# Layer 1 of a graph network on one core: TensorE in the order of tracing, and the attention bias moved behind the division

## Chip, cores and metric
The kernel runs on one core of a Trainium2 chip. The metric is device time in microseconds (us) from launch to end; lower is better. Beside the runs there is one execution under the hardware profiler, whose page and trace are quoted. PE is the matrix engine TensorE (PEld its weight loads), DVE is VectorE, ACT is ScalarE, POOL is GpSimd, SP is SyncE, which here only issues transfers.

## The reference, cut to what matters
Two layers work on x of shape 32 x 512 x 256 (32 batches of 512 nodes) with an integer adjacency adj of 32 x 512 x 512. Each has a graph part and a feed-forward part, each added to x after a layer norm. The change touches only layer 1:

```python
# graph part: attention over the adjacency, 4 heads of 64; adj is 0 or 1
h = einsum('bnd,hde->bhne', layernorm(x), W)
weight = leaky_relu(e_src + e_dst), or -1e9 where adj == 0
attention = softmax(weight)
dst = einsum('bhij,bhje->bhie', attention, h) + bias
out = relu(dst) + h
out = (out - mean(out)) / sqrt(var(out) + 1e-6) * ln_gamma + ln_beta
x = x + out
# feed-forward part
sw = softmax((layernorm(x) @ W_x.T @ W_slice.T + ...) / temp)    # 8 heads of 64 slices
st = slices: sum over nodes of fx * sw, over the sum of sw
ot = a state-space scan over the 64 slices (convolutions, silu, softplus, decay matrices)
x = x + (ot spread back through sw) @ out_w.T + out_b
```

The weights of an attention row sum to one after the division, so the bias may be added to the values before the weighted sum or to the divided result after it.

## The kernel before
The program runs layer 0 (`layer0_sorted`) and then layer 1 (`layer1_plain`); a second pair of functions follows under a condition that is false for these inputs. Instructions are recorded by Python generators. A scheduler then places them on each engine: it takes an instruction when its inputs are ready by its own model of time, with the order of recording as the priority. So the order on an engine can differ from the order in which the code was traced.

Layer 1 takes 32 batches, two to a group, 16 groups. Two streams are woven together when they are recorded. One is `mixer(g)`, the feed-forward part of a group: `slices` for its first and its second batch, then `tokens`, `scan`, and `unslice` for both. The other is `attentions()`, which runs two batches ahead: `attention(b)` woven with `prepare(b + 1)`. The loop at the end (L1589 to L1597) advances the attention by credits: each step of `mixer` yields a weight `want`, and every full credit (`want * PACE`) runs one step of `attentions`. `STEPS` (L890) is the number of steps of `prepare`; it enters both `woven` and `PACE`.

`prepare(b)` gathers x by four indirect transfers issued from POOL (L1154), normalises it into the buffer of the values hv (ACT, L1133, after the statistics on DVE, L1126, and a power on POOL, L31), transposes it on PE (x3T, L1142, copied out by ACT, L1143) and multiplies it with the weights (hp, L1180, four tiles). ACT copies each tile to ht (L1186) and forms exponentials. POOL then adds the bias for all four tiles, from ht into hv (L1189), and DVE multiplies hv by an exponential in four steps (L1202). The logits of the rows are transposed (minep, L1193), written to memory and read back as four broadcast tiles `own` through SP (L1197, L1200). It also turns the adjacency into a mask (maskp L1084 on PE, cast by DVE L1085).

`attention(b)` forms the weights `att` on DVE (L1213), sums them with the values on PE (avp L1249, adp L1254: a "turn" is one row tile of all four heads), copies the sums out, transposes them back (dp, bp, L1232) and divides on DVE (L1275). `norm(b, av)` follows in three pieces: relu plus h (L1290), sum (L1292) and mean, subtraction (L1294), square on ACT (L1296), sum (L1298) and small steps (L1299), a power on POOL (L1300), multiplication by gamma (L1301) and by that power (L1303), and the addition to x (L1304).

`slices(b)` transposes x (x4T), computes logits (lgp, L1335, four tiles) and their exponential on ACT (L1336), normalises them on DVE (sw: L1337, L1340, L1341, L1342), and sums x over them on PE (yTp, L1347: two banks c of four tiles t, t inside c); swp (L1352) transposes sw. `tokens` and `scan` are one dependent chain: uTp, rnp, xp (L1400), bcp (L1409), dtp, zp (L1393); softplus and convolutions on DVE and ACT with several function tables; then gp (L1487), segp (L1491), xtp, qp, yp (L1517), yTp (L1527), oTp (L1535), vp (L1557); `unslice` computes outp (L1567), adds it to x (L1569) and writes the output. PSUM tiles of layer 1 share two tags of four banks, "any" and "pv".

Of the kernel before, what the change touches and what calls it, by code (L numbers as in the profile page):

```python
# [19 lines left out]
P = 128  # L20
N = 512
D = 256
NT = N // P
# [841 lines left out]
def layer1_plain(tc, ident, eps, x2s, ranks, adj, w, out, over, ps):  # L865
# [3 lines left out]
    nc = tc.nc  # L869
    B = adj.shape[0]  # L870
    SEG = B // len(x2s)
    GB = 2
    AH, _, HO = w["W"].shape
# [13 lines left out]
    HE = HO + 1  # L887
    AP = AH // 2
    TURNS = AP * NT + 6
    STEPS = 15  # L890
    WANTED = 68
    AHEAD = 3
    ATT = 2 * (AHEAD + 2) + AP + 1
# [7 lines left out]
    with ExitStack() as ctx:  # L901
# [246 lines left out]
        def prepare(b):  # L1148

            while b >= AHEAD_X and b - AHEAD_X not in stored:  # L1150
                yield True
            xt = xs[b] = sb.tile([P, NT, D], F32, tag="x", name=f"x{b}", bufs=AHEAD_X)
            for t in range(NT):
                nc.gpsimd.indirect_dma_start(  # L1154
                    out=xt[:, t, :], out_offset=None, in_=x2s[b // SEG],
                    in_offset=bass.IndirectOffsetOnAxis(
                        ap=ranks[:, b * NT + t : b * NT + t + 1].bitcast(U32), axis=0))

            hv = sb.tile([P, NT, AH, HE], F32, tag="hv", name=f"hv{b}")
            xn = hv.rearrange("p t h e -> p (t h e)")[:, : NT * D].rearrange("p (t d) -> p t d", t=NT)  # L1160
            edged = masks(b) if b not in masked else range(3)
            for i, _ in enumerate(edged):
                if i < 3 or b not in masked:
                    yield
                if i == 2:
                    normed(xt, xn, f"c{b}")
                    nc.gpsimd.tensor_add(xt, xt, beta.unsqueeze(1).to_broadcast([P, NT, D]))
                    yield
            mask = masked.pop(b)
            xnT = yield from turned(xn, "x3T", f"x3T{b}")  # L1170
            yield


            ht = sb.tile([P, NT, AH * HO], F32, tag="ht", name=f"ht{b}")
            other = sb.tile([P, NT, AH], F32, tag="other", name=f"other{b}")
            mine = sb.tile([P, AH, NT], F32, tag="mine", name=f"mine{b}")
            for t in range(NT):
                ph = psum("any", f"hp{b}_{t}")
                for c in range(DC):
                    nc.tensor.matmul(ph[:, : AH * (HO + 2)], xnT[:, c, t * P : (t + 1) * P], wa[:, c, :],  # L1180
                                     start=c == 0, stop=c == DC - 1)
                d = ph[:, AH * HO : AH * HO + AH]
                nc.scalar.activation(mine[:, :, t], ph[:, AH * (HO + 1) : AH * (HO + 2)], AF.Exp, scale=1.0 - SLOPE)
                nc.scalar.activation(hv[:, t, :, HO], d, AF.Exp)
                nc.scalar.activation(other[:, t, :], d, AF.Exp, scale=SLOPE - 1.0)
                nc.scalar.copy(ht[:, t, :], ph[:, : AH * HO])  # L1186
                yield

            nc.gpsimd.tensor_add(hv[:, :, :, :HO], ht.rearrange("p t (h e) -> p t h e", h=AH),  # L1189
                                 abias.rearrange("p (h e) -> p h e", h=AH).unsqueeze(1).to_broadcast([P, NT, AH, HO]))  # L1190
            yield
            pt = psum("any", f"minep{b}")
            nc.tensor.transpose(pt[: AH * NT, :P], mine.rearrange("p h t -> p (h t)"), ident)  # L1193
            row = sb.tile([AH * NT, P], F32, tag="turned", name=f"turned{b}", bufs=1)
            nc.scalar.copy(row, pt[: AH * NT, :P])
            own_row = dr.tile([AH, N], F32, tag="own", name=f"ownd{b}")
            nc.sync.dma_start(own_row.rearrange("h (t p) -> (h t) p", p=P), row)  # L1197
            own = [wide("own", f"own{b}_{h}", AH + 1) for h in range(AH)]
            for h in range(AH):
                nc.sync.dma_start(own[h], own_row[h].partition_broadcast(P))  # L1200
            for t in range(NT):
                nc.vector.tensor_mul(hv[:, t, :, :HO], hv[:, t, :, :HO], hv[:, t, :, HO:].to_broadcast([P, AH, HO]))  # L1202
            ready[b] = mask, ht, hv, other, own
            yield

# [10 lines left out]
        def attention(b):  # L1216

            mask, ht, hv, other, own = ready[b]
            xt = xs[b]
            av = sb.tile([P, NT, AH, HO], F32, tag="av", name=f"av{b}", bufs=1)  # L1220
            turns = [(q, j) for j in range(NT) for q in range(AP)]

            def begin(b, n):
                q, j = turns[n]
                if (b, 2 * q, j) not in weighed:
                    weigh(b, q, j)

            def back(src, kind):

                dst = psum("pv", f"{kind}{b}")  # L1230
                for t in range(NT):
                    nc.tensor.transpose(dst[:, t * P : (t + 1) * P], src[:, t * P : (t + 1) * P], ident)  # L1232
                return dst

            for n in range(AHEAD):
                begin(b, n)
            pv = [psum("pv", f"avp{b}_{q}") for q in range(AP)]
            for i, (q, j) in enumerate(turns):
                if i + AHEAD < len(turns):
                    begin(b, i + AHEAD)  # L1240
                elif b + 1 in ready:
                    begin(b + 1, i + AHEAD - len(turns))

                if q + 1 == AP:
                    ends = dict(start=j == 0, stop=j == NT - 1)
                    for p in range(AP):
                        for k in range(2 * HO // HW):
                            h, e = 2 * p + k * HW // HO, k * HW % HO
                            nc.tensor.matmul(pv[p][k * HW : (k + 1) * HW, :], hv[:, j, h, e : e + HW],  # L1249
                                             weighed[b, h, j], **ends)  # L1250
                    if j == 0:
                        pd = psum("pv", f"adp{b}")
                    for h in range(AH):
                        nc.tensor.matmul(pd[h * HW : (h + 1) * HW, :], hv[:, j, h, HO:].to_broadcast([P, HW]),  # L1254
                                         weighed.pop((b, h, j)), **ends)
                yield
                if unfinished and i != 2:
                    next(unfinished[0], None)
                    yield
                    if i > 2:  # L1260
                        unfinished.pop()
            dT = wide("att", f"adT{b}", ATT)
            nc.scalar.copy(dT, pd)
            vT = [wide("att", f"avT{b}_{q}", ATT) for q in range(AP)]
            for q in range(AP):
                nc.scalar.copy(vT[q], pv[q])
            yield
            dt = back(dT, "dp")
            rs = sb.tile([P, NT, AH], F32, tag="rs", name=f"rs{b}")
            nc.vector.tensor_scalar_max(rs, dt.rearrange("p (t h e) -> p t h e", t=NT, h=AH)[:, :, :, 0], 1e-30)  # L1270
            nc.vector.reciprocal(rs, rs)
            for q in range(AP):
                bt = back(vT[q], f"bp{q}_")
                heads = slice(2 * q, 2 * q + 2)
                nc.vector.tensor_mul(av[:, :, heads, :], bt.rearrange("p (t h e) -> p t h e", t=NT, h=2),  # L1275
                                     rs[:, :, heads].unsqueeze(3).to_broadcast([P, NT, 2, HO]))
                yield
            unfinished.append(norm(b, av))

# [293 lines left out]
        def mixer(g):  # L1573
            uT = sb.tile([P, KC, GB * G], F32, tag="uT", name=f"uT{g}", bufs=1)
            yT = sb.tile([P, DC, H, GB, G], F32, tag="yT", name=f"yT{g}", bufs=1)
            rn = sb.tile([P, GB, KC], F32, tag="rn", name=f"rn{g}")
            sws = []
            for j in range(GB):
                sws.append((yield from slices(g * GB + j, j, yT, rn)))
            yield 3  # L1580
            tokens(g, yT, rn, uT)
            v = yield from scan(g, uT)
            yield 2
            for j in range(GB):
                unslice(g * GB + j, sws[j], v[:, j])
                yield 2
# [1 line left out]

        ahead = attentions()  # L1589
        credit = 0.0  # L1590
        for g in range(B // GB):
            for want in mixer(g):
                credit += want * PACE
                while credit >= 1.0:
                    credit -= 1.0
                    if next(ahead, True):
                        credit = 0.0  # L1597


        flags = over[:, 2 * AH + 3 :]  # L1600
# [639 lines left out]
```

## Time and profile before

| what | value |
|---|---|
| runs | 4453.05, 4452.75, 4458.42 us; median 4453.05 |
| the profiled execution's own time | 4459.08 us |
| its span, first to last instruction | 4456.4 us, mean granted PE clock 0.948 |
| PE busy | 3922.0 us, 88% |
| PEld busy | 2470.6 us, 55% |
| DVE busy | 3347.2 us, 75% |
| ACT busy | 2291.6 us, 51% |
| POOL busy | 1718.8 us, 39% |
| transfers | 474.21 MB, mean 106 GB/s |
| last piece of layer 0 on PE, first of layer 1 | 2363.84 and 2384.94 us |

The profile has a page with busy times, the span in 40 slices, and the costliest groups of instructions. Further views of the same trace are the table of waits (who stood still for whom), the timeline (instructions in order, equal neighbours merged, with the idle time before a piece and what ended it in brackets), and the busy time of each engine within chosen stretches. A PE count of the profile is twice the number of matmuls in f32, since each matmul leaves two records; transposes through f32 leave one. A group of layer 1 lasts about 126 us.

### The profile page before, as it was taken

Reading aid. Unit: us, or ns where it says so; the run is one execution under the profiler, and the core shown is the slowest. Engines: PE = TensorE matmul, PEld = TensorE weight load, DVE = VectorE, ACT = ScalarE, POOL = GpSimd, SP = SyncE. Lnnn points to the kernel's source line nnn. Section 1 sums busy time; section 2 is a strip of 40 time slices with the busy share of each in tenths; the row PEclk is TensorE's granted clock in tenths of the full one; section 3 lists DMA queues with packets and bytes.
Section 4 is the critical chain, followed back from the end, with each engine's and each line's share of the span. In section 5 each row is a group of like instructions: output and inputs, shape, how many; then the busy total and the mean of one; then the engine's idle time right before and its main releaser. Section 6 shows DMA issues by size and latency. Waiting matters only on the chain.

```text
span 4456.4 us, 57911 instructions
## 1 busy us (share of the span) xinstructions
PE 3922.0 (88%) x20311; PEld 2470.6 (55%) x20311; DVE 3347.2 (75%) x7008; ACT 2291.6 (51%) x4756; POOL 1718.8 (39%) x2036
## 2 busy tenths in 40 slices
PE   5568898899988999888997899999999999999987
PEld 4454565566656656545554455555555555555555
DVE  6668887897788987877766777767677877778763
ACT  3345565566564665556654544544545444454433
POOL 2357644664446644454314232332222232332220
PEclk8679999999999999989998999999999999999998
DMA  5546543664436543564422111111111111111100
GB/s 133 160 144 223 190 130 122 210 200 139 156 117 213 187 147 129 162 201 167 138 81 67 36 53 57 56 48 58 51 43 42 53 55 55 58 48 58 41 15 16
DMA packets 235107, 474.21 MB, mean 106 GB/s; under 512 B 38299, under 2 KB 114075, under 8 KB 234804
## 3 DMA queue, kind: packets, MB, share of 16 engines
q0 software_dynamic: 98688, 315.94, 22.2%
q1 hardware_dynamic: 136116, 154.46, 11.0%
q8 instruction: 162, 2.65, 0.2%
q14 instruction: 141, 1.16, 0.1%
HBM read 413.16 MB, written 57.16 MB: 106 GB/s over the span
## 4 chain that ended last, share of the span: by engine, by line
DVE 34%; PE 32%; DMA 11%; issue 9%; POOL 9%; ACT 5%; SPq 0%; POOLq 0%; DVEq 0%; ACTq 0%
DVE att L1213 5%; DVE acc L637 4%; PE clsp L623 3%; PE avp L1249 3%; PE po L652 3%; PE gatep L623 3%; DMA rows<-table,xs 2%; PE yTp L1347 2%; DVE sw L1337 2%; DVE sw L1342 2%; DVE best L598 2%; DMA rows<-table,tops 2%; DVE sst L1340 2%; DMA best<-table,xs 2%; PE xp L1400 1%
## 5 line engine op out<-in xcount | busy, mean ns | idle before, releaser
L623 PE MATMUL clsp<-xnT,wc 128*128 128x512 f32 x1024 | 520.8, 627 | 49.7 <-ACT cls L625 37.6
L623 PE MATMUL gatep<-xnT,wg 128*128 128x512 f32 x1024 | 499.8, 607 | 10.5 <-ACT gate L625 7.7
L652 PE MATMUL po<-wd,acc 128*128 128x256 f32 x2048 | 455.4, 381 | 6.1 <-DVE acc L641 3.8
L1213 DVE SCALAR_TENSOR_TENSOR att<-own,other,mask 128x512 f32<-128x512 f32 x512 | 392.9, 796 | 79.0 <-DMA own<-ownd 79.0
L652 PEld LDWEIGHTS po<-wd,acc 128*128 128x128 f32 x2048 | 388.3, 191 | 72.1 <-issue 9.2
L598 DVE SCALAR_TENSOR_TENSOR best<-rows,xs,best 128x1024 f32<-128x1024 f32 x212 | 274.4, 1295 | 121.9 <-ACT best L592 76.4
L637 DVE SCALAR_TENSOR_TENSOR acc<-past,fld,acc 128x512 f32<-128x512 f32 x448 | 345.7, 775 | 24.9 <-ACT past L636 16.9
L632 ACT ACTIVATE acc<-tz,fld 128x512 f32<-128x512 f32 x256 | 198.8, 777 | 269.3 <-PE tz L630 240.1
L623 PEld LDWEIGHTS gatep<-xnT,wg 128*128 128x128 f32 x1024 | 196.0, 196 | 252.3 <-issue 197.9
L636 ACT ACTIVATE past<-tz,fld 128x512 f32<-128x512 f32 x448 | 291.4, 693 | 68.1 <-DVE acc L637 66.6
L1347 PE MATMUL yTp<-sw,x 128*128 128x512 f32 x512 | 264.6, 655 | 64.3 <-DVE sw L1342 59.6
L595 POOL DMA_INDIRECT rows<-table,xs x212 | 249.5, 1177 | 171.6 <-DVE best L598 119.0
L1249 PE MATMUL avp<-att,hv 128*32 128x512 f32 x2048 | 298.9, 607 | 5.6 <-DVE att L1213 5.6
L623 PEld LDWEIGHTS clsp<-xnT,wc 128*128 128x128 f32 x1024 | 181.5, 198 | 188.1 <-issue 111.8
L434 PE MATMUL pm<-h,adj 128*128 128x258 f32 (+1 forms) x1024 | 181.2, 324 | 99.9 <-DVE keep L427 33.7
L1300 POOL TENSOR_TENSOR mu<-mu,eps 128x16 f32<-128x16 f32 x32 | 111.6, 3487 | 391.1 <-DVE mu L1299 391.0
L1335 PE MATMUL lgp<-wsl,x4T 128*128 128x512 f32 x512 | 242.8, 613 | 15.7 <-ACT sw L1336 6.8
L1154 POOL DMA_INDIRECT x<-x2s,ranks x128 | 135.9, 1062 | 298.1 <-DVE att L1213 148.1
L625 ACT ACTIVATE gate<-gatep,fld 128x512 f32<-128x512 f32 x256 | 175.5, 685 | 142.6 <-PE gatep L623 123.8
L553 POOL DMA_INDIRECT xs<-rows_of,order x128 | 156.1, 1219 | 221.5 <-DVE acc L637 100.8
L1567 PE MATMUL outp<-v,swT 128*128 128x256 f32 x1024 | 227.6, 381 | 0.0
L625 ACT ACTIVATE cls<-clsp,fld 128x512 f32<-128x512 f32 x256 | 176.1, 688 | 93.9 <-PE clsp L623 55.6
(599 smaller groups left out, 8978.1 us busy)
## 6 DMA issues: line engine op xcount, KB each, us to landing
adj<-in_adj POOLq DMA_DIRECT2D x128, 256.0 KB
ai<-in_adj SPq DMA_DIRECT2D x128, 256.0 KB
own<-ownd SPq DMA_DIRECT2D x128, 256.0 KB
rows_of<-keep SPq DMA_DIRECT2D x32, 550.0 KB
x<-in_x SPq DMA_DIRECT2D x32, 512.0 KB
x2s<-xs SPq DMA_DIRECT2D x32, 512.0 KB
out<-x SPq DMA_DIRECT2D x32, 512.0 KB
rows<-table,xs POOLq DMA_INDIRECT x212
```

The source lines that it names most:

```text
L595: nc.gpsimd.indirect_dma_start(out=row, out_offset=None, in_=table, in_offset=bass.IndirectOffsetOnAxis(ap=idxs[:, k : k + 1].bitcast(U32) ...
L598: nc.vector.scalar_tensor_tensor(m, row, vals[:, k : k + 1], m, ALU.add, ALU.max)
L623: nc.tensor.matmul(pf, wf[:, c, f * P : (f + 1) * P], xnT[:, c, :], start=c == 0, stop=c == DC - 1)
L625: nc.scalar.activation(o, pf, fn, bias=fld[:, f, bf : bf + 1], scale=1.0 if fn == AF.Gelu else 0.5)
L636: nc.scalar.activation(r, z, AF.Relu, bias=fld[:, f, AT + b : AT + b + 1])
L637: nc.vector.scalar_tensor_tensor(y, r, fld[:, f, CH + b : CH + b + 1], y, ALU.mult, ALU.add)
L652: nc.tensor.matmul(po[:, i, :], acc[f][:, t * P : (t + 1) * P], wd[:, f, :], start=f == 0, stop=f == FC - 1)
L1213: nc.vector.scalar_tensor_tensor(e, own[h], other[:, j, h : h + 1], mask[:, j, :], ALU.max, ALU.mult)
L1249: nc.tensor.matmul(pv[p][k * HW : (k + 1) * HW, :], hv[:, j, h, e : e + HW], weighed[b, h, j], **ends)
L1335: nc.tensor.matmul(pf, xnT[:, c, t * P : (t + 1) * P], wsl[:, c, :], start=c == 0, stop=c == DC - 1)
L1347: nc.tensor.matmul(py, xn[:, t, c * P : (c + 1) * P], sw[:, t, :], start=t == 0, stop=t == NT - 1)
L1567: nc.tensor.matmul(po[:, :D], swT[:, k, t * P : (t + 1) * P], v[:, k, :], start=k == 0, stop=k == KC - 1)
```

## The change
Three edits, all in layer 1. First, the loop that records layer 1's two streams is put under a manual schedule for PE alone: PE's instructions keep the order of tracing, and the scheduler still places those of the other engines. Second, the bias leaves the preparation of the values: DVE now multiplies ht by the exponential straight into hv, one tile behind the copy of the tile, and one yield is gone from `prepare`; the bias is added on POOL to the divided result, once for each pair of heads. Third, `STEPS` falls from 15 to 14 with the yield.

```diff
-    STEPS = 15
+    STEPS = 14
...
+            def values(t):
+                nc.vector.tensor_mul(hv[:, t, :, :HO], ht[:, t, :].rearrange("p (h e) -> p h e", h=AH),
+                                     hv[:, t, :, HO:].to_broadcast([P, AH, HO]))
...
                 nc.scalar.copy(ht[:, t, :], ph[:, : AH * HO])
+                if t:
+                    values(t - 1)
                 yield
-            nc.gpsimd.tensor_add(hv[:, :, :, :HO], ht.rearrange("p t (h e) -> p t h e", h=AH),
-                                 abias.rearrange("p (h e) -> p h e", h=AH).unsqueeze(1).to_broadcast([P, NT, AH, HO]))
-            yield
+            values(NT - 1)
...
-            for t in range(NT):
-                nc.vector.tensor_mul(hv[:, t, :, :HO], hv[:, t, :, :HO], hv[:, t, :, HO:].to_broadcast([P, AH, HO]))
...
                 nc.vector.tensor_mul(av[:, :, heads, :], bt.rearrange("p (t h e) -> p t h e", t=NT, h=2),
                                      rs[:, :, heads].unsqueeze(3).to_broadcast([P, NT, 2, HO]))
+                nc.gpsimd.tensor_add(av[:, :, heads, :], av[:, :, heads, :],
+                                     abias.rearrange("p (h e) -> p h e", h=AH)[:, heads, :].unsqueeze(1)
+                                     .to_broadcast([P, NT, 2, HO]))
                 yield
...
-        for g in range(B // GB):
-            for want in mixer(g):
-                credit += want * PACE
-                while credit >= 1.0:
-                    credit -= 1.0
-                    if next(ahead, True):
-                        credit = 0.0
+        with tc.manual_schedule(engines={mybir.EngineType.PE}):
+            for g in range(B // GB):
+                for want in mixer(g):
+                    credit += want * PACE
+                    while credit >= 1.0:
+                        credit -= 1.0
+                        if next(ahead, True):
+                            credit = 0.0
```

## The prediction
> **What bounds the kernel now.** I read the page's busy table and slices first: PE is busy 88% of the 4456.4 us span and 9 tenths in nearly every slice of layer 1 (from about 2375 us). So I cut one steady group of layer 1 (two batches, 3027.3 to 3153.7) into stretches at PE's landmarks and asked for busy time in each (us of the stretch; PE, PEld, DVE, ACT, POOL busy with counts; granted clock; DMA share; GB/s):
> ```profile
> 3027.30:3047.80 20.50, 20.31 (x210) 15.03 (x209) 15.60 (x41) 11.50 (x23) 3.56 (x3) 1.00 0.04 14
> 3047.80:3053.70 5.90, 5.90 (x61) 1.97 (x58) 5.90 (x16) 5.78 (x12) 0.00 (x0) 1.00 0.00 0
> 3053.70:3082.90 29.20, 28.17 (x215) 20.88 (x212) 12.31 (x31) 16.78 (x51) 6.74 (x6) 1.00 0.21 65
> 3082.90:3119.60 36.70, 31.29 (x154) 16.77 (x153) 32.90 (x60) 12.21 (x29) 16.56 (x12) 1.00 0.28 86
> 3119.60:3153.70 34.10, 31.23 (x139) 15.23 (x138) 24.94 (x55) 14.96 (x45) 9.50 (x7) 0.90 0.10 32
> ```
> PE works 116.9 of 126.4 us: 9.5 us idle a group, nearly all in the last two stretches, where the slice softmax (sw) of the first and second batch feeds yTp. If all that idleness went, 16 groups would give 152 us: the ceiling of any gain. The waits (2540 to 4400; engine, line, for whom: us, times, longest) say whose it is:
> ```profile
> PE yTp L1347 <- DVE sw L1342: 57.7, 34, 3.0
> PE oTp L1535 <- ACT yT L1529: 14.0, 15, 1.1
> DVE hv L1202 <- POOL hv L1189: 158.2, 28, 8.9
> DVE att L1213 <- DMA own<-ownd: 79.0, 15, 7.3
> ```
> DVE stands 158 us behind the bias add, 5.6 us each time, with the sw work queued behind it. PE's own waits are small because its order was placed around late results. The clearest place is the second stretch: between the end of zp and gp the scheduler put masks and two turns of avp/adp (PE's timeline, pieces):
> ```profile
> 3044.14 3.68 PE L1393 MATMUL zp<-inT,uT 128*128 128x512 f32 x8
> 3047.66 0.83 PE L1084 MATMUL maskp<-identb,a 128*128 128x128 bf16 x12
> 3048.42 1.49 PE L1249 MATMUL avp<-att,hv 128*32 128x512 f32 x11
> ...
> 3053.71 0.46 PE L1487 MATMUL gp<-cpad,bcT 64*64 64x64 f32 x8
> ```
> ACT needs just that time for gp's inputs:
> ```profile
> 3047.86 0.60 ACT L1450 ACTIVATE z<-zp 128x512 f32<-128x512 f32 x1 [0.39 <-PE zp L1393]
> ...
> 3048.76 1.28 ACT L1443 ACT_TABLE_LOAD   x1
> ...
> 3050.30 1.28 ACT L1455 ACT_TABLE_LOAD   x1
> ...
> 3052.20 0.39 ACT L1462 ACTIVATE cpad<-bcT,bc_b 64x128 f32<-64x128 f32 x1
> ```
>
> **What the Trainium skill says.** "TensorE: Matmul & The Clock Gate", section "Architectural detail", has ACT and DVE as strict FIFOs; the trace agrees: at 3093.8 ACT stood 6.59 us before the normalisation of hv, while the first lgp ended at about 3098 and its exp, queued behind, started at 3102.42. The same page's "Part 1: The HAM clock gate" halves PE's clock after an idle window of about 3.4 us; the trace agrees: after 9.97 us idle at 2408.74, eight 128x128 transposes took 1.97 us, against 1.04 us at 3091.34. "ScalarE: Activation LUTs", "What ACT_TABLE_LOAD costs", gives 1283 ns a load and a drain of about 1380 ns; the trace shows 1283 ns, the next ACTIVATE starting at once, so I use 1.28.
>
> **The change, part by part** (per group; 14 of the 16 groups are of the steady kind; T is zp's end, W the end of the first batch's outp, 3082.9 above).
>
> *zp to gp.* The built order of the changed kernel has, in 11 of 14 groups, zp, three mask transposes, gp: both avp/adp turns (5.2 us above) have gone to before vp and after qp. In 3 groups one turn (2.7 us) stays. gp's inputs hang on ACT: after T come z 0.6, load 1.28, log 0.23, load 1.28, three silus and two for bcT/cpad, 1.5: T+4.9, as before (3052.6 less 3047.8). PE's masks end at T+0.66, so it waits 4.3 us; segp then waits for seg on DVE, 0.7 more (seg ended T+6.6 before). In 8 groups z stands ahead of the log, 5.0 us; in 3, one silu is already done, 4.5; in the 3 with a turn between, about 1. Sum 8x5.0 + 3x4.5 + 3x1 = 56 us. The bounds are 25 (if exp and log finish before zp) and 75. What hid this was the avp work; its new places need no cover: vp waited 1.6 us in the whole window. yTp to oTp keeps its 0.9.
>
> *Order within tiles.* Before, hp's first halves of three tiles run ahead of the second x3T copy; now hp_0 needs both at once. x3T was copied 3.5 us after the last yTp, PE comes there after swp 1.85, x3T 0.5, half of hp_0 0.45: wait 0.7. x3T to hp_0 after qp likewise, 0.7, of which the rests overlap: I take 1.0, and 0.25 where lgp follows x4T directly: 1.25x14 = 18 us (0 to 28).
>
> *Bias moved; first batch (fourth stretch).* Removed: 32 POOL adds of 2.36 us and their wait. Added: 64 POOL adds of half the width, about 1.2 us (half of 2.36), between the division (L1275) and the relu (L1290). DVE's busy time is the same. POOL now adds at about W+2.8 to W+5.4, ahead of the four gathers of x for the next batch, which started at W+5.7 before (3088.61): they are hardly later. The third thing is the order on DVE: the norm's multiplication by mu (L1303) stood behind all sw work of this batch; now it stands before it, or amid it, in every steady group. It needs the pow on POOL, and that is queued behind k, one to four, of the next gathers:
> ```profile
> 3226.87 1.02 POOL L1154 DMA_INDIRECT x<-x2s,ranks  x1 [0.19 <-issue]
> 3228.19 1.50 POOL L1154 DMA_INDIRECT x<-x2s,ranks  x1 [0.30 <-issue]
> 3230.00 2.23 POOL L1154 DMA_INDIRECT x<-x2s,ranks  x1 [0.30 <-issue]
> 3232.53 0.95 POOL L1154 DMA_INDIRECT x<-x2s,ranks  x1 [0.30 <-issue]
> 3233.50 3.34 POOL L1300 TENSOR_TENSOR mu<-mu,eps 128x16 f32<-128x16 f32 x1
> ```
> A gather is about 1.3 us with its gap. Counting DVE's rows from W (division 3.4; relu after POOL at 5.4; statistics after the fourth gather's landing, 12.4; ht reduction and the small pow, 15.4), the norm's multiply can run at 15.4 + 1.3k + 3.4, and the last sw is ready 12 us later (multiply, att, add 3.1; sw rows at 0.6 each and two mask casts, 9.0): W+36.1 for k=4, 33.5 for k=2, 32.2 for k=1. PE's last five yTp add 4.3 (3.5 us for four, at 3116.03), so the stretch ends at W+40.4, 37.8 or 36.5 instead of 36.7. With four groups of k=4, four of k=2, two of k=1 and four in which the multiply stands amid the sw rows, taken like k=2: (4x3.7 + 8x1.1 - 2x0.2)/14 = about +1.5 us, 21 us in all (-5 a group if DVE were not blocked; +4 if every group had k=4).
>
> *Second batch (fifth stretch).* The wait of hv for POOL is gone (7.6 us at 3006), so the first two sw come early. But two att rows stand ahead of the third or fourth sw in DVE's order and need own, which lands about 9 us after its row: PE's wait goes from 2.9 to about 2.4: -7 us (-40 to +15).
>
> *Clock.* Stalls of 4 to 9 us let the clock fall more often; the fifth stretch above shows 0.90 after gaps of 2.1 and 2.9 us. I take 1 us a group, 14 us (0 to 40). STEPS from 15 to 14 removes one empty step: the pace stays. The start and the tail of layer 1 change by -15 to +15: the first attention must wait for own with nothing ahead of it, but the second batch's masks no longer come first; 0.
>
> Sum: 56+18+21-7+14 = +102 us on the profiled execution: 4456.4+102 = 4558 span, 4459.1+102 = 4561 with what lies around it. The median of the runs is 6 us below the profiled run: 4555.
>
> **The rivals.** (1) Faster. One mechanism: DVE, freed of the hv wait, delivers sw in time. If the norm's multiply does not block, the first sw is ready at about W+20 and the fourth stretch falls to its 31.3 us of PE work, the fifth to 31.2: -8 a group, -112 over 14; against it 56+18: -38, so 4459-38-6 = 4415. It decides once these two stretches give back more than 5.3 us a group. For it: the 158 us; against: DVE's order and the 3.34 us pow. (2) Much slower: the pow waits behind four gathers in nearly every group (+4 instead of +1.5), two stalls a group let the clock fall (+3 instead of +1): 102 + 2.5x14 + 2x14 + 19 for the first term at its upper bound = +184, so 4459+184-6 = 4637. For it: DVE's order; against: PE's own order still holds avp turns to slip. (3) No net effect: gains in the sw stretches of 5 us a group eat the first term, 4453; nothing in the order favours just that.
>
> **How the numbers follow.** Likeliest 0.55 (4500 to 4610), rival 1 0.2, rival 2 0.2, rival 3 0.05. Range 4420 to 4640: it reaches into rivals 1 and 2. Faster by over 0.2% (about what a measurement of this kernel can tell) 0.2, within 0.05, slower 0.75.
>
> **What would show it.** Right: PE waits of 4 to 5 us before gp for ACT's cpad, new in the table of waits, 45 to 65 us together; DVE waiting for POOL's mu, tens of us where it was 23.6; hv's 158 us gone; yTp's wait for sw as large as before or larger; layer 0 unchanged to 2375. Wrong: no wait before gp (then ACT finished earlier than its loads allow), or yTp's waits gone.

## The result, and the profile after

The changed kernel takes 4692.93 us (median of 4 runs, 4688.68 to 4698.1) against 4452.9 (4450.26 to 4458.42): a ratio of 1.0538, with an interval of 1.052 to 1.0556. It is 240 us slower; the forecast was 102 us slower (4555), with 4640 as the upper end. Its profiled execution spans 4696.4 us at a mean granted PE clock of 0.928, where before had 4456.4 and 0.948. PE is busy 85% (3971.7 us), DVE 73%.

The same steady group as before, cut at the same landmarks (us of the stretch; PE, PEld, DVE, ACT, POOL busy with counts; granted clock; DMA share; GB/s):

```profile
3110.30:3131.40 21.10, 19.43 (x206) 14.71 (x205) 19.48 (x45) 10.75 (x22) 3.54 (x2) 1.00 0.04 14
3131.40:3136.90 5.50, 0.80 (x15) 0.66 (x13) 5.43 (x16) 5.43 (x11) 0.10 (x1) 0.93 0.00 0
3136.90:3176.07 39.17, 37.95 (x262) 24.02 (x263) 17.86 (x38) 17.60 (x53) 4.75 (x5) 0.88 0.16 48
3176.07:3221.40 45.33, 34.71 (x153) 17.74 (x152) 32.67 (x66) 12.64 (x29) 20.67 (x16) 0.89 0.24 70
3221.40:3252.40 31.00, 28.46 (x138) 14.18 (x137) 21.62 (x38) 14.77 (x45) 8.97 (x6) 1.00 0.11 35
```

The group has grown from 126.4 to 142.1 us. In the second stretch PE is busy 0.80 us of 5.50, where it was busy all the time: that is the forecast wait before gp. What the forecast priced at no more than 1 us a group is the clock: its column has 0.88 and 0.89 in the third and fourth stretches, where both were 1.00. The fourth stretch is 8.6 us longer than before, and PE works 34.71 us of it instead of 31.29, though there is no more to compute.

PE's waits in layer 1 (2400 to 4640; who stood for whom: us, times, longest):

```profile
PE yTp L1354 <- DVE sw L1349: 56.9, 37, 8.2
PE maskp L1084 <- DVE mask L1085: 29.2, 7, 8.0
PE rnp L1379 <- DVE rn L1362: 24.4, 7, 4.1
PE avp L1252 <- DVE att L1216: 21.4, 2, 11.0
PE yTp L1354 <- DVE mask L1085: 21.0, 4, 9.4
PE gp L1494 <- DVE la L1474: 18.8, 4, 4.7
PE gp L1494 <- DVE att L1216: 18.8, 4, 4.7
PE lgp L1342 <- DVE mask L1085: 17.4, 5, 5.7
...
PE gp L1494 <- issue: 13.4, 3, 4.6
...
PE gp L1494 <- ACT cpad L1469: 12.6, 3, 4.2
```

And DVE's in the same window:

```profile
DVE hv L1179 <- ACT ht L1191: 189.2, 89, 9.2
DVE av L1310 <- POOL mu L1307: 83.2, 29, 6.4
```

The four rows of gp add up to 63.6 us in 14 waits. The table names la, att and cpad in turn, because those that ended last lie close together; they are one wait. gp reads bcT and cpad, which ACT makes, and DVE's rows beside ACT's chain end at nearly the same time. The wait for sw is as large as it was, but the three rows with "mask" hold 67.6 us, where the same rows had 4.4 before. DVE's wait for the bias is not gone: it has become one for ACT's copy ht. And DVE now waits 83.2 us for mu, where it waited 26.0 before.

To have averages and not one group, I cut the 13 groups from the second to the fourteenth at PE's landmarks and took the length, PE's idle time, and the time that the trace's record of the granted clock has at half speed (us a group; the record knows only full and half). PE works 4.68 us of a group at half clock before and 15.26 after. Half of that is my estimate of what the clock costs, 2.3 and 7.6 us, as the same work takes about twice as long there (lines in experiment 3).

| from, to | before: length, idle, half clock | after: length, idle, half clock |
|---|---|---|
| first uTp, zp's end | 20.04, 0.91, 1.05 | 21.34, 3.19, 3.15 |
| zp's end, segp | 6.45, 0.00, 0.00 | 6.65, 4.79, 1.13 |
| segp, yp | 8.02, 0.12, 0.00 | 11.09, 0.47, 6.48 |
| yp, last outp | 28.75, 1.09, 0.00 | 34.60, 0.63, 0.00 |
| last outp, swp of the first batch | 29.85, 4.45, 1.05 | 36.40, 8.94, 8.93 |
| that swp, next uTp | 31.69, 2.06, 2.89 | 30.36, 1.94, 0.00 |
| the group | 124.79, 8.63, 4.99 | 140.45, 19.97, 19.69 |

Of the 15.66 us that a group has gained, 11.34 are idle time and 5.29 slower clock; PE's work at full clock is 0.97 less. (Single stretches also change because work has moved: between yp and outp stands 6 us more of it, without any idleness.) The rest of the 240 us: from layer 1's first PE instruction to the first uTp 156.7 us against 141.7, +15.0. Layer 0 ended 7.7 us later in this execution (2382.55), though nothing in it was changed; in the run with the order alone, below, it ended at 2374.88 as before. It counts as the spread of one execution: over all the profiles here layer 0, the same in each, ends between 2368.6 and 2387.7 us.

### The profile page after: what moved, and what is told of

Same layout as the page of the kernel before. It is cut to its first block, busy times and chain, and to the rows that moved or that the text cites. A ratio compares the mean times of both kernels' runs of the same rounds, so it can differ in the third digit from the quotient of the medians.

```text
span 4696.4 us, 57968 instructions
## 1 busy us (share of the span) xinstructions
PE 3971.7 (85%) x20311; PEld 2486.5 (53%) x20311; DVE 3424.4 (73%) x7008; ACT 2293.4 (49%) x4756; POOL 1746.7 (37%) x2068
## 4 chain that ended last, share of the span: by engine, by line
PE 36%; DVE 30%; DMA 10%; issue 8%; POOL 8%; ACT 7%; SPq 0%; another core or an unknown queue 0%; POOLq 0%; DVEq 0%; ACTq 0%
PE avp L1252 4%; DVE att L1216 4%; PE clsp L623 4%; DVE acc L637 3%; PE gatep L623 3%; DMA rows<-table,xs 3%; PE hp L1185 2%; DVE best L598 2%; PE yTp L1354 2%; PE outp L1574 2%; DVE sw L1344 2%; PE po L652 2%; DMA rows<-table,tops 2%; POOL x L1154 2%; PE adp L1257 2%
## 5 line engine op out<-in xcount | busy, mean ns | idle before, releaser
L1252 PE MATMUL avp<-att,hv 128*32 128x512 f32 x2048 | 276.2, 659 | 21.4 <-DVE att L1216 21.4
L1342 PE MATMUL lgp<-wsl,x4T 128*128 128x512 f32 x512 | 257.8, 642 | 33.2 <-DVE mask L1085 17.4
L434 PEld LDWEIGHTS pm<-h,adj 128*128 128x128 f32 x1024 | 149.3, 210 | 127.6 <-issue 70.9
L1179 DVE TENSOR_TENSOR hv<-ht,hv 128x256 f32<-128x256 f32 x128 | 77.1, 621 | 189.4 <-ACT ht L1191 189.2
```

The costliest lines, as they stand in the source:

```text
L434: nc.tensor.matmul(pm[:, : c1 - c0], a[:, i, t * P : (t + 1) * P], h[:, i, c0:c1], start=i + c0 == 0, stop=i + 1 == NT and c0 > 0)
L1342: nc.tensor.matmul(pf, xnT[:, c, t * P : (t + 1) * P], wsl[:, c, :], start=c == 0, stop=c == DC - 1)
```

## The experiments

My theory at first was that nearly all comes from PE's fixed order: the bare wait before gp and what the clock does after it. The rival was the moved bias, with DVE's multiplication by mu standing in front of the sw work until the pow on POOL is done.

**1. The order alone.** The kernel before, with

```diff
-        for g in range(B // GB):
+        with tc.manual_schedule(engines={mybir.EngineType.PE}):
+            for g in range(B // GB):
```

> The kernel before with TensorE's fixed order alone; the bias stays where it was (added to ht ahead of the hv multiply), 15 steps. Theory 1 (the 240 us come from TensorE's fixed order: the uncovered wait before gp, the slow clock after it, the waits for sw): 4640 to 4700, with some 60 us of waits before gp. Theory 2 (they come from the moved bias: VectorE's multiply by mu sits ahead of the sw chain and waits for the pow behind the gathers): 4500 to 4540, little more than the 64 us of waits before gp.

4709.47 us, ratio 1.0574 (1.0545 to 1.0602). The order alone costs 254 us, no less than both edits together (the median is 16 us higher, but the two intervals overlap). Its first two waits of PE:

```profile
PE yTp L1347 <- DVE sw L1342: 68.4, 35, 6.5
PE gp L1487 <- ACT cpad L1462: 59.5, 14, 5.1
```

A group takes 141.76 us here, with 20.11 idle and 22.32 at half clock. The start of layer 1 is 15.8 us longer, as in the kernel after, so that part belongs to the order. But DVE waits 60.4 us for mu here too (26.0 in the kernel before), with the bias in its old place: the rival's mechanism does not need the moved bias. With PE's order fixed, the scheduler also placed DVE's, ACT's and POOL's instructions in another order, so this run prices the fixed order together with what follows from it on the other engines.

**2. The bias alone.** The kernel after, with that line and its indentation taken out again.

> The kernel after without the fixed order of TensorE; the moved bias and the 14 steps stay. Theory 1 (order): 4430 to 4470, no gp wait, since the scheduler puts attention turns between zp and gp as before. Theory 2 (moved bias): 4560 to 4640, with a wait of VectorE for mu of some 80 us as in the kernel after.

4557.76 us, ratio 1.0234 (1.0209 to 1.0259): +103 us, and of gp's waits only the single one of 4.4 us that the kernel before has too. The moved bias costs too, but the two costs do not add up: 254 + 103 is 357, both edits give 240. The view of DVE's waits shows one reason:

```profile
DVE av L1310 <- POOL mu L1307: 82.3, 28, 6.4
```

That is the 83.2 us of the kernel after. The stretch from outp to swp has 34.93 us here, 34.73 with the order alone, 36.40 with both: each edit alone brings DVE into much of the same stall, and it can be brought there only once. That is not all of it. The groups grow by 17.0 us with the order alone, by 6.5 with the bias alone and by 15.7 with both, 7.8 less than the sum; 3.4 of these lie in that stretch. Another 2.3 lie between uTp and zp's end, which the order alone lengthens to 22.69 us and both edits only to 21.34; why is open.

**3. Does the clock cost anything, or only the wait?**

```diff
             pg = psum("any", f"gp{g}")
+            for _ in range(9):
+                nc.tensor.matmul(pg[:, 2 * G :], inT[:, 0, :P], inT[:, 0, : N - 2 * G], start=True, stop=True)
```

> The kernel after with nine matmuls of 128x384 before gp, into columns of gp's tile that nobody reads (about 4.0 us by zp's 592 ns for 512 columns), so that TensorE works through most of the wait. They change no result. If the slow stretch after the wait (segp 2.48 us for four against 1.42, avp 3.64 against 1.92 in one group) comes from TensorE having stood idle, those durations fall back, and 14 groups x 4.3 us = 60 us go: 4620 to 4650. If the clock falls for another reason, or the slow stretch hides a wait that then appears: 4690 to 4720.

4660.91 us, ratio 1.0467 (1.0441 to 1.0492): 32 us gained by added work. PE's timeline of the group around the wait, in the kernel after:

```profile
3136.88 0.70 PE L1494 MATMUL gp<-cpad,bcT 64*64 64x64 f32 x8 [4.70 <-DVE att L1216]
3137.97 2.48 PE L1498 MATMUL segp<-seg,seg_l 128*64 128x512 f32 x4 [0.38 <-DVE seg L1488]
...
3142.93 3.64 PE L1252 MATMUL avp<-att,hv 128*32 128x512 f32 x16
```

and here:

```profile
3115.54 6.07 PE L1493 MATMUL gp<-inT 128*128 128x384 f32 x18 [0.34 <-DVE mask L1085]
3121.54 0.45 PE L1496 MATMUL gp<-cpad,bcT 64*64 64x64 f32 x8
3121.93 1.08 PE L1500 MATMUL segp<-seg,seg_l 128*64 128x512 f32 x4
...
3124.31 1.92 PE L1252 MATMUL avp<-att,hv 128*32 128x512 f32 x16
```

segp falls from 2.48 to 1.08 us and the 16 avp records from 3.64 to 1.92: the same instructions at full clock. Between segp and yp no half clock is left (6.48 us in the kernel after), and that stretch is 3.5 us shorter. The gain fell short of the forecast 43 to 73 us because I had sized the filler wrongly: I took 592 ns for a matmul, but each leaves two records, and nine of them took 6.07 us. They reach past the wait, and the stretch from zp to segp grew by 1.2 us.

**4. The same with four matmuls**, which leave about 2 us of idle time.

> The kernel after with four unread matmuls of 128x384 before gp instead of nine (1.8 us by zp's rate): TensorE still stands still for some 2.9 us before gp. If the length of the single pause sets the slow clock (pauses up to 3.0 us were followed by 3.4 us at half clock, pauses of 4 us and more by 6.8 to 10.2 us): half-clock time from zp's end to yp falls from 7.6 us per group to 3.4 or less, and the time to 4665 to 4680. If every pause costs the same: no gain, 4690 to 4700.

4665.76 us, ratio 1.0476 (1.0447 to 1.0505): 27 us gained. Busy time and clock of PE in the same two pieces of the group (zp's end to segp, segp to yp):

```profile
3127.50:3134.00 6.50, 4.02 (x30) 1.00 0.00 0
3134.00:3142.00 8.00, 7.76 (x52) 1.00 0.13 36
```

PE stands still 2.5 us of the 6.50, and the clock stays at 1.00. On average 0.8 us of half clock is left from zp's end to yp, of 7.6. In this group the longest pause is 1.56 us, where it was 4.70. So breaking up the pause does about as well as filling it: the 5 us between the two runs are no more than two runs of one and the same program differ by in experiment 9. Whether the longest pause decides, or the sum of the idle time, this does not tell apart, since both have shrunk.

**5. A real cover for the wait.** Steps of the attention are moved from ahead of yp to ahead of gp:

```diff
                 nc.vector.tensor_mul(heads(seg[j]), per_head(la[:, j, :]), per_slice(seg_r))
-            yield 7
+            yield 10
...
-            yield 7
+            yield 4
             py = psum("any", f"yp{g}")
```

> The kernel after with three of the mixer's turns moved from ahead of yp to ahead of gp (7 and 7 become 10 and 4): one attention turn and one or two turned columns of x3T now stand between zp's masks and gp, with the same sum per group. If the wait before gp and its clock fall are real losses: minus 64 us of waits and up to 60 us of slow clock, 4570 to 4630. If the wait merely moves to yp, whose cover is cut: 4670 to 4700, with a wait of 4 us before yp.

4688.38 us, ratio 1.0523 (1.0493 to 1.0552): no gain to speak of. gp's waits fall to 16 us, but yp's take their place:

```profile
PE yp L1524 <- DVE mix L1517: 33.9, 14, 3.7
...
PE gp L1494 <- ACT cpad L1469: 10.0, 10, 1.5
```

The half clock has only moved: 7.0 us a group now lie between yp and outp, where there was none. The wait moved to the next link of the same chain. The scheduler's order had covered both gaps (0.12 us of idle time a group from zp's end to yp). A likely reason, not tested here, is that it could spread avp turns by need, while the order of tracing puts a turn at one place or another.

**6. The pow left out**, in the kernel after and in the kernel with the bias alone:

```diff
-            nc.gpsimd.tensor_tensor(mu[:, 1, :], mu[:, 1, :], eps[:, 1:2].to_broadcast([P, NG]), ALU.pow)
```

> The kernel after without the norm's inverse square root on GpSimd (L1307 is left out: the result is multiplied by the variance). VectorE's multiply by mu then waits for nothing of GpSimd. If that wait (83 us in 29 waits) makes the fourth stretch long: the stretch from the last outp to the first swp falls from 36.4 us to about 30 as before the change, 14 x 6.5 = 91 us, 4600. If the fixed order makes that stretch long by itself (the run with the order alone has 34.7 us there and no moved bias): 4650 to 4690.

> The kernel with the moved bias alone (TensorE as the scheduler places it), also without the norm's inverse square root. If the wait for mu behind the gathers is the price of the moved bias: the 5.1 us per group that the fourth stretch has gained go, 14 x 5.1 = 71 us, 4470 to 4490. If the moved bias costs by something else (the hv multiplies spread over the tile loop, the added GpSimd instructions): 4530 to 4560.

4627.41 us (ratio 1.0387, 1.0355 to 1.0419) and 4490.53 us (1.0075, 1.0051 to 1.0099): 66 and 67 us less than with the pow. The stretch from outp to swp falls from 36.40 to 32.61 and from 34.93 to 31.22. Two thirds of the moved bias's 103 us go with this one power and the wait for it. In the first kernel 2.8 us a group stay in that stretch, so neither of the two expectations for it holds alone.

**7. Both: nine matmuls before gp, and no pow.**

> The kernel after with both: nine unread matmuls before gp, and the norm's inverse square root left out. If the two costs are separate, the gains add up: 4661 minus what the run without the pow gains over the kernel after; with 91 us, 4570. If the slow clock of one stretch carries into the next, the two together gain more than the sum; below 4550. If one wait only hides another: 4630 or more.

4606.65 us, ratio 1.033 (1.0299 to 1.0362). The gains of 32 and 66 would give 4595; they add up to within 11 us, so the two costs are nearly separate. Half clock is down to 5.8 us a group, close to before's 5.0. Of the 9.1 us a group that are left over before, 5.2 are more work for PE, mostly the filler, and 3.8 idle time, mostly the waits of rnp and the masks.

**8. The bias's addition left out.**

> The kernel after without the added bias (the two GpSimd additions of 1.28 and 1.72 us per slice are left out; hv is made of ht without bias as in the kernel after). If the additions' place in the chain av, bias, relu, mu costs: VectorE's waits for av (20 us in 16) and 3 us ahead of each norm go, 10 to 30 us, 4665 to 4685. If they are what pushes mu's pow behind the gathers: 60 us or more, under 4635. If they are hidden: 4685 to 4700.

4651.72 us, ratio 1.044 (1.0416 to 1.0465): 41 us less, between the two expected values. DVE's wait for mu stays (85.1 us), so the additions do not push the pow behind the gathers. The gain is spread over two stretches (1.7 us a group before zp, 1.6 after outp); which link of the chain makes it stays open.

**9. The hv multiplications after the loop over tiles**, in the kernel after and in the kernel with the bias alone:

```diff
-                if t:
-                    values(t - 1)
                 yield
 
-            values(NT - 1)
...
+            for t in range(NT):
+                values(t)
             ready[b] = mask, ht, hv, other, own
```

> The kernel after with the four hv multiplies traced after the loop over tiles, where the kernel before had them (still from ht, without the bias). If VectorE's waits for ht inside the loop (189 us in 89) delay the mask copies and sw for which TensorE waits: those waits go, 20 to 60 us, 4635 to 4675. If they are idle time of VectorE that costs nothing: 4685 to 4700. If the four multiplies in one piece stand in front of the masks instead: above 4700.

> The kernel with the moved bias alone, and with its four hv multiplies after the loop over tiles. The run without the pow left 33 us above the kernel before. If the spread multiplies are these 33 us: 4520 to 4530. If the moved bias costs through mu's place in the queues alone: 4550 to 4565. If the multiplies' place also decides how early the norm runs, and so whether mu meets the gathers: below 4510.

4686.53 us (1.0521, 1.0489 to 1.0554) and 4554.6 (1.022, 1.019 to 1.025). Against 4692.93 and 4557.76 that is nothing to speak of, and it could not be more: the edit changed the order of tracing, but the scheduler placed the instructions of every engine in the same order as without it. DVE's wait for ht is there again:

```profile
DVE hv L1179 <- ACT ht L1191: 189.7, 89, 9.2
```

So each of the two kernels was measured twice, with 6 and 3 us between the medians, and the multiplications were not tested. What can be read from the trace of the kernel after is this. PE's waits for DVE add up to 249 us; when each is followed back through DVE's unbroken work to the pause ahead of it, none begins at a wait for ht. That speaks against a cost of the 189 us but does not show it. The 33 us that the bias still cost without the pow stay open too. The additions on POOL, worth 41 us in experiment 8, are one candidate; they were not left out in the kernel with the bias alone.

**10. A pow that POOL does not do.** Nine matmuls before gp, and

```diff
-            nc.gpsimd.tensor_tensor(mu[:, 1, :], mu[:, 1, :], eps[:, 1:2].to_broadcast([P, NG]), ALU.pow)
+            nc.scalar.activation(mu[:, 1, :], mu[:, 1, :], AF.Sqrt)
+            nc.vector.reciprocal(mu[:, 1, :], mu[:, 1, :])
```

> The kernel after with nine unread matmuls before gp, and with the norm's inverse square root as a square root on ScalarE and a reciprocal on VectorE in place of the pow on GpSimd: all work is done. With the pow left out this was 4607. If ScalarE has room (49% busy): 4605 to 4625. If its table loads (1.28 us each, two more per slice) delay x4T or the exponentials of sw: 4640 to 4680, with longer waits of TensorE for ScalarE.

4622.83 us, ratio 1.0373 (1.0343 to 1.0402): with the whole norm computed it is 38 us less than the filler alone, and 16 more than the filler with no pow at all. It is the fastest complete kernel with the fixed order, and still 170 us above before. No version here beat the kernel before.

## Why the prediction was wrong

The sign, the place and the mechanism of its first term were right. Its sum failed in two terms and missed two others. All per group, times 14 as the prediction had it:

- **zp to gp: forecast 56 us, measured 63.6 in gp's waits** and 67 in idle time up to segp. ACT's chain is as it was worked out: z at 3131.76, two loads of 1.28 us, cpad done at 3136.78.
- **Clock: forecast 14 us, measured 74** (5.29 x 14, an estimate as above). This term failed most. The prediction looked at what followed gaps of 2.1 and 2.9 us (0.90 in one stretch of 34.1 us, which is 3.4 us of lost clock by itself) and took 1 us a group for gaps of 4 to 9. The measured relation is steeper: in before, 18 of the 26 half-clock times of layer 1 lasted 3.4 us, after pauses up to 3.0 us; in the kernel after, pauses of 4 us and more were followed by 6.8 or 10.2 us in most cases. One wait of 4.7 us before gp costs 4.7 us and then, on average, about half of the 6.9 us that PE works at half clock up to yp. Experiments 3 and 4 show it: with the same wait filled or halved the half clock behind it is gone, and 32 and 27 us come back. The Trainium skill, "TensorE: Matmul & The Clock Gate", section "HAM oscillation — how this bites in real kernels", describes this loss for a matmul loop that waits about 3 to 5 us for a transfer each time, and takes half of the throttled time as the penalty; this trace agrees: the 16 avp records take 3.64 us behind the wait and 1.92 where it is filled. The prediction cited that page for the fall of the clock and did not carry out its sum.
- **Order within tiles: forecast 18 us.** hp's wait for x3T was 15.8 us in 26; right in size.
- **First batch: forecast 21 us, measured 63 of idle time**, and with it 7.9 us a group more at half clock. (The forecast's own terms give 23, not 21.) The forecast mechanism is there. POOL's and DVE's timelines in the group above:

```profile
3199.03 0.94 POOL L1154 DMA_INDIRECT x<-x2s,ranks  x1 [0.30 <-issue]
3199.99 2.94 POOL L1307 TENSOR_TENSOR mu<-mu,eps 128x16 f32<-128x16 f32 x1
3202.90 2.36 POOL L1167 TENSOR_TENSOR x<-x,beta 128x1024 f32<-128x1024 f32 x1
```

```profile
3202.96 3.39 DVE L1310 TENSOR_TENSOR av<-av,mu 128x1024 f32<-128x1024 f32 x1 [6.43 <-POOL mu L1307]
...
3212.50 0.68 DVE L1085 CAST mask<-maskp 128x512 uint8<-128x512 bf16 x1
```

  The pow starts the moment the fourth gather is issued, DVE stands 6.43 us, and then the multiplication takes 3.39 us where 1.22 is usual. PE's longest pause in this group, 6.61 us before yTp, ends with sw. In the previous group the longest pause, 8.01 us, ends with a mask:

```profile
3060.64 1.22 DVE L1310 TENSOR_TENSOR av<-av,mu 128x1024 f32<-128x1024 f32 x1 [4.52 <-POOL mu L1307]
3061.78 0.68 DVE L1085 CAST mask<-maskp 128x512 uint8<-128x512 bf16 x1
```

```profile
3062.51 0.58 PE L1084 MATMUL maskp<-identb,a 128*128 128x128 bf16 x4 [8.01 <-DVE mask L1085]
```

  What the step left out is who else waits behind the multiplication. The prediction followed sw alone; but sw's wait in this stretch rose only from 2.1 to 2.6 us a group. The new 4.8 us are for the mask casts (before: 0.3). maskp fills a bank of the tag "any", which only the cast frees; maskp, lgp and yTp all draw on these four banks, and the cast is queued on DVE behind the multiplication. Followed back as in experiment 9, 81 us of PE's waits begin at DVE's wait for mu: 34 of those for sw and 47 of the 50 that maskp and yTp spend on masks. lgp's 17.4 us for masks are another matter. They do not begin there, and they stay the same without the pow (1.34 us a group); the order alone has 1.63 of them and the bias alone 0.22, so they belong to the order.
- **Second batch: forecast -7 us, measured -2** of idle time. "The wait of hv for POOL is gone" was wrong: the multiplications wait for ht instead, 189.2 us. Whether that costs anything was not shown (experiment 9).
- **uTp to zp: not in the sum, measured 32 us** of idle time. rnp waits 24.4 us for rn, which DVE makes after ACT's last swT: a fixed order has nothing to put there, and the prediction, which looked for bared waits at gp and hp, passed by this one.
- **Start: forecast 0 (-15 to +15), measured +15**, in both kernels with the fixed order and not without it: avp waits twice for att, 21.4 us together, before with 5.6.

Forecast idle terms (56 + 18 + 21 - 7) are 88 us; the measured idle time is 11.34 x 14 = 159. With the clock's 74, the start's 15, layer 0's 8 and 14 us less of work at full clock it makes 242, against 240 of the two spans.

Rival 2, with its pow behind the gathers and two falls of the clock a group, was the nearest, at 4637, and still 56 us short. Rival 1 failed at its own point: the sw stretches gave nothing back. What also failed is the picture that lies under both: that the two edits have separate prices. Together they cost no more than the order alone.

## What to carry to other kernels

A kernel whose chain is kept covered by a scheduler's choice can lose that cover at several places at once when one engine's order is fixed: list every link of the chain that has a latency of its own (here gp, yp, rnp, the first attention), and not only the one where the cover is best to be seen. Price a pause of a few us on PE with the time at half clock behind it; breaking it up may pay as much as removing it. After an edit, check in the trace that the order on the engine you meant has changed: a scheduler may place the same program as before. When an in-order engine stalls, ask for each queued instruction which buffer it would have freed, and not only which result it would have made.

## What the hardware showed that I had not expected

The half-clock times come in steps: 3.41, 6.83, 10.24, 13.65, 17.07 and 20.48 us in layer 1; the two exceptions are the last ones of the two executions. The Trainium skill, "TensorE: Matmul & The Clock Gate", section "Part 1: The HAM clock gate", gives a window of 3413 ns and half clock after an idle window; the steps agree. But pauses of 1.6 to 3.0 us, shorter than the window, were also followed by a time of one such step at half clock, 18 times in layer 1 of the kernel before. How often depends on the pause. Of the pauses there that began at full clock, from 2440 us to the last 60 us, half clock followed none of 16 of 1.0 to 1.5 us, 1 of 10 up to 2.0, 2 of 7 up to 2.5 and 15 of 18 up to 3.0; in the kernel after, it followed all 29 of 4 us and more.

DVE's multiplication by mu took 1.22 us in 26 of 32 cases, and 3.38 in the six in which POOL's addition L1167 (2.36 us) ran beside it; in the kernel before, no case met it. The hv multiplication went from 0.42 to 2.25 us in the 14 cases beside POOL's addition L1335. Beside POOL's gathers there was no difference (1.22 in six cases). The Trainium skill, "SBUF — State Buffer", section "SBUF: two separate sides", has a port pair that a DVE instruction with two inputs in SBUF and a GpSimd instruction that reads SBUF take in turns, one waiting out the other's whole instruction. The numbers agree: the excess of 2.2 and 1.8 us is most of POOL's instruction (2.36 us). That the port is the cause is the page's statement; no experiment here tested it. The 14 cases are why the mean of the hv multiplication rose from 420 to 621 ns.
